# Comparison numbers and W2 of an edge network in PSUM, a table loop in two halves, and one-hot numbers made first

## The chip, the cores and the metric

The kernel runs on one core of a Trainium2 chip. It is written with a tile framework: the program names tiles in SBUF and PSUM and the operations on them, the framework puts each engine's instructions into one static order and sets the semaphores between the engines. The engines are TensorE (PE in the profile, its weight loads PEld), VectorE (DVE), ScalarE (ACT), GpSimd (POOL) and SyncE (SP), and each works through its own list in order. [...]

The metric is the device time of one execution in microseconds (us), taken as a median over executions. The profile is of one further execution, whose own time is given beside it.

## The reference

Four graph networks run one after the other on 6250 nodes of 128 features, each on the layer norm and ReLU of the running sum `x`, and each adds its result to `x`. The graph has 106250 edges, sorted by destination.

```python
def net0(h, norm, rel_emb, W_neighbor, loop_weight, src, dst, edge_type):   # relations, 500 types
    msg = (h[src] + rel_emb[edge_type]) @ W_neighbor
    return relu(segment_sum(msg, dst) * norm + h @ loop_weight)

# net1: three layers; mean over the neighbours, a router takes 2 of 8 experts for every node,
#       h = h + conf * moe; the result is h @ W_out + b_out

def net2(x, src, dst, W1, b1, W2, b2, W4, b4):                              # edge network
    theta = x[dst] - x[src]
    w = sigmoid(relu(theta @ W1 + b1) @ W2 + b2)                            # one number per edge
    agg = segment_sum(w * theta, dst)
    return agg + indegree * (x @ W4 + b4)

# net3: three layers of l2norm(mean over the neighbours) @ Wl.T + bl + l2norm(x) @ Wr.T

x = x + net0(relu(layernorm(x)), ...)
x = x + net1(relu(layernorm(x)), ...)
x = x + net2(relu(layernorm(x)), ...)
x = x + net3(relu(layernorm(x)), ...)
```

## The kernel before

Nodes are padded to 49 tiles of 128, and these are grouped into 13 blocks of four tiles (the last block has one tile). `blk_tiles(b)` is the number of tiles of a block, `P` = `D` = 128, `BW` = 512. Edges are padded to 832 chunks of 128; four chunks make a group, so there are 208 groups (`NWG`) of 512 edges. Since the edges are sorted by destination, the destinations of a group lie in a window of 128 rows (`win(g)`).

**Net 0 and the adjacency.** The kernel first writes the adjacency matrix as bytes into HBM (`adj`), block of destinations by block, from the last block (12) down to block 0. SP clears the blocks from a tile of zeros (`clear`, L310 to L317). VectorE finds for each edge the place of its byte and the number of equal edges: `keys_of(q)` (L398 to L423) loads, on the queue of ScalarE, the source and destination numbers of four index groups of 2048 edges (52 such groups in all), and forms a key for each edge; a copy of the middle of the keys, `own_key`, goes into the PSUM tile `seen`, made by ScalarE (L413). `places(s)` (L425 to L455) compares each key with its neighbours (`req`, L433) and computes the indices `ixs` in a dozen small VectorE instructions. GpSimd then scatters: `scatter(s)` (L457 to L467) issues 16 indirect DMAs of 128 places, one byte each, for one index group, 832 in all, from block 12 down to block 0. The `places` stand in a high-priority part, so the framework puts them early in VectorE's list. TensorE multiplies block b of `adj` with the node rows as soon as SP has loaded it back (`aggregate`, L262 to L282).

Net 0 also needs the counts of edge types. `seen` holds a table of the numbers 0 to 511 (`iota_t`, in bf16): GpSimd makes the numbers (`rnum_i`, L359), VectorE turns them into the bit pattern of small floats (`as_number`, L328) and casts them (L362), TensorE transposes them into `seen` (L364). VectorE compares with it to form one-hot rows (`ohd`, L512, and `oht`, L516). The biases of all networks are loaded by short DMAs on GpSimd's queue (`bias_rows`, L184 to L198): those of `gbias` first; those of net 1's layers belong to net 1's code, and the framework's list has those of the first layer, and some of the second, ahead of the first scatter (L192, between 54 and 79 us in the trace).

**Net 1** takes the adjacency through three layers with gathers and expert multiplies. It isn't touched by the change, but for the place of its bias DMAs on GpSimd's queue.

**Net 2, tables.** A loop over the 13 blocks (L949 to L996) does for each block, in the order of the program: load `rres` (net 1's result, 256 wide) and `rxb`; transpose `rres` on TensorE (L963) and copy it to `roT` (L964); multiply with `W_out` into `rpo` and add a bias row (L968, L970); add it to `rxb` (L971); layer norm of the block's rows into `rh2` (`norm_rows`, L230 to L246, in which VectorE and ScalarE alternate); transpose these (`transposed`, L291, L292); two multiplies per tile, with W1 into `rpg` (L979) and with W4 into `rpv` with a bias row (L980, L981); copy `rpg` to `rgs_o` on ScalarE (L983); write `rh2` and `rgs_o` into the table `tab_s` in HBM (L984, L985); add b1 and split into three bf16 parts (L987, `split3` L123 to L130) for the table `tab_d` (L991); and `rv2` = `rpv` times the in-degree plus `rxb`, which goes to `x_d[1]` (L993 to L996). The framework's list for TensorE keeps this order, so the transposes of a block's `rh2` stand between its `rpo` and its `rpg`.

**Net 2, edges.** For each of the 208 groups (L1089 to L1129) GpSimd gathers four chunks of 128 rows of `tab_s` by source number (L1096, tiles `rss`, six of them in turn). VectorE makes `ohT` (a one-hot of destinations, L1101) and `oh` (L1104, 128x1024, which compares the numbers 0 to 255 of `iota2` with `tloc`); TensorE brings the destinations' rows from the window of `tab_d` (`pz`, L1109); VectorE forms `rz` = `pz` - `rss` and then `max(rz, 0) * W2`:

```python
nc.vector.tensor_tensor(z, pz, ss[:, :, 1 + D:], ALU.subtract)                       # L1111
nc.vector.scalar_tensor_tensor(z, z, 0.0, w2b[:, None, :].to_broadcast([P, WG, D]),  # L1112
                               op0=ALU.max, op1=ALU.mult)
```

ScalarE sums each chunk (L1116) and takes the sigmoid (L1118); ScalarE and VectorE scale the gathered rows into `mv` (L1122, L1123); TensorE adds them into the PSUM tiles `acc` with `oh` (L1129). At the last group of a tile `finish` (L1062 to L1085) turns `acc` into rows of `x` and of the next network. Once enough blocks of these are ready, each group is also followed by one or two steps of `some_sources` (L1043 to L1060): a part of net 3's first multiply, which casts a stretch of `adj` on ScalarE (L1051) and multiplies it on TensorE (L1054, `rpart`). `iota2` (L1026) and `w2b` (L1010) are SBUF tiles. The PSUM pools of this part are `ps_z` 2, `ps_acc` 4 and `ps_a2` 2 tiles, eight banks in all.

**Net 3** is three layers of `aggregate` with small multiplies (L1136 on). It isn't touched.

Of the kernel before, what the change touches and what calls it, by code (L numbers as in the profile page):

```python
# [133 lines left out]
def regular_path(ctx: ExitStack, tc: tile.TileContext, i: dict, out: bass.AP):  # L134
# [167 lines left out]
    with ExitStack() as prep:  # L302
# [6 lines left out]
        pp = pool("rprep", 1)  # L309
        p2 = pool("rprep2", 2)  # L310
        zn = NT * BW // 4
        zero = pp.tile([P, zn // 4], F32, name="rzero")
# [11 lines left out]


        typ_f = pp.tile([P, NCH], F32, name="typ_f")
        dloc_f = pp.tile([P, NCH], F32, name="dloc_f")

        def as_number(dst, k):

            nc.vector.tensor_scalar(dst, k, 16, 1 << 30, op0=ALU.logical_shift_left, op1=ALU.bitwise_or)

        with tc.tile_pool(name="rcols", reuse_waits="tile", bufs=1) as cp:
# [18 lines left out]
            nc.sync.dma_start(dst16, dst_h)  # L352

        ps_k = pool("ps_k", 1, space=bass.MemoryType.PSUM)
        seen = ps_k.tile([P, BW], F32, name="seen")
        iota_t = seen[:, 0:TYP // 2].bitcast(BF16)
        with tc.tile_pool(name="rnum", reuse_waits="tile", bufs=1) as cp:
            num = cp.tile([P, TYT, P], I32, name="rnum_i")
            nc.gpsimd.iota(num, pattern=[[P, TYT], [0, P]], base=0, channel_multiplier=1)  # L359
            as_number(num, num)  # L360
            num_b = cp.tile([P, TYT, P], BF16, name="rnum_b")
            nc.vector.tensor_copy(num_b, num.bitcast(F32))  # L362
            for q in range(TYT):
                nc.tensor.transpose(iota_t[:, q * P:(q + 1) * P], num_b[:, q, :], ident_b)  # L364
        rel3 = pp.tile([P, TYT, 3, D], BF16, name="rel3")
# [32 lines left out]
        def keys_of(q):  # L398
# [13 lines left out]
            own = slice(HALO, HALO + GJ)  # L412
            nc.scalar.copy(own_key[q % 2], key[:, :, own])  # L413
            t1 = p2.tile([P, QG, GJ], I32, name="w_t1")
# [526 lines left out]
    with tc.tile_pool(name="rl2n", reuse_waits="tile", bufs=2) as lp, \  # L941
            tc.tile_pool(name="ps_m2", reuse_waits="tile", bufs=8, space=bass.MemoryType.PSUM) as ps_m:
        w_out = lp.tile([P, 2, D], F32, name="rw_out", bufs=1)
        nc.scalar.dma_start(w_out, rows_of(i["L1_gnn_W_out"], 0, 2))
        w1 = lp.tile([P, D], F32, name="rw1", bufs=1)
        nc.scalar.dma_start(w1, i["L2_gnn_W1"])
        w4 = lp.tile([P, D], F32, name="rw4", bufs=1)
        nc.scalar.dma_start(w4, i["L2_gnn_W4"])
        b1b = lp.tile([P, D], F32, name="rb1b", bufs=1)  # L949
        nc.scalar.dma_start(b1b, bcast_rows(i["L2_gnn_b1"], 0, D))  # L950
        for b in range(NBLK):
            nt = blk_tiles(b)
            w = nt * P
            ts = slice(4 * b, 4 * b + nt)
            res = lp.tile([P, 4, H], F32, name="rres", bufs=4)
            nc.sync.dma_start(res[:, :nt], rows_of(hf_d, 4 * b, nt))
            xb = lp.tile([P, 4, D], F32, name="rxb")
            nc.scalar.dma_start(xb[:, :nt, :], rows_of(x_d[0], 4 * b, nt))
            oT = lp.tile([P, 2, BW], F32, name="roT")
            for f in range(2):  # L960
                p = ps_m.tile([P, 4, P], F32, tag="mm", name="rtr4")
                for t in range(nt):
                    nc.tensor.transpose(p[:, t, :], res[:, t, f * P:(f + 1) * P], ident)  # L963
                nc.scalar.copy(oT[:, f, :w], p[:, :nt, :].rearrange("p t d -> p (t d)"))  # L964
            po = ps_m.tile([P, 4, D], F32, tag="mm", name="rpo")
            for t in range(nt):
                for f in range(2):
                    nc.tensor.matmul(po[:, t, :], oT[:, f, t * P:(t + 1) * P], w_out[:, f, :],  # L968
                                     start=(f == 0), stop=False)
                nc.tensor.matmul(po[:, t, :], sel(1), gbias[:, :D], start=False, stop=True)  # L970
            nc.vector.tensor_tensor(xb[:, :nt, :], po[:, :nt, :], xb[:, :nt, :], ALU.add)  # L971
            norm_rows(h2[:, ts], xb[:, :nt], nt, lp)
            hT = lp.tile([P, BW], F32, name="rhT2")
            transposed(hT, h2, b, ps_m)
            pg = ps_m.tile([P, 4, D], F32, tag="mm", name="rpg")
            pv = ps_m.tile([P, 4, D], F32, tag="mm", name="rpv")
            for t in range(nt):
                tl = hT[:, t * P:(t + 1) * P]
                nc.tensor.matmul(pg[:, t, :], tl, w1, start=True, stop=True)  # L979
                nc.tensor.matmul(pv[:, t, :], tl, w4, start=True, stop=False)  # L980
                nc.tensor.matmul(pv[:, t, :], sel(3), gbias[:, :D], start=False, stop=True)  # L981
            gs = lp.tile([P, 4, D], F32, name="rgs_o")
            nc.scalar.copy(gs[:, :nt], pg[:, :nt])  # L983
            nc.sync.dma_start(rows_of(tab_s, 4 * b, nt)[:, :, 0:D], h2[:, ts, :])  # L984
            nc.sync.dma_start(rows_of(tab_s, 4 * b, nt)[:, :, D:], gs[:, :nt])  # L985
            gd = lp.tile([P, 4, D], F32, name="rgd_o")
            nc.vector.tensor_tensor(gd[:, :nt], gs[:, :nt], b1b[:, None, :].to_broadcast([P, nt, D]), ALU.add)  # L987
            gd3 = lp.tile([P, 4, 3, D], BF16, name="gd3")
            split3(nc, gd3[:, :nt, 0, :], gd3[:, :nt, 1, :], gd3[:, :nt, 2, :], gd[:, :nt],
                   lp, [P, nt, D], "gdr")  # L990
            nc.sync.dma_start(rows_of(tab_d, 4 * b, nt), gd3[:, :nt].rearrange("p t s f -> p t (s f)"))  # L991
            v = lp.tile([P, 4, D], F32, name="rv2")
            nc.vector.tensor_tensor(v[:, :nt], pv[:, :nt],  # L993
                                    deg_r[:, ts][:, :, None].to_broadcast([P, nt, D]), ALU.mult)
            nc.vector.tensor_tensor(v[:, :nt], xb[:, :nt], v[:, :nt], ALU.add)
            nc.scalar.dma_start(rows_of(x_d[1], 4 * b, nt), v[:, :nt])  # L996


# [7 lines left out]
    with tc.tile_pool(name="rl2e", reuse_waits="tile", bufs=2) as ep, \  # L1006
            tc.tile_pool(name="ps_z", reuse_waits="tile", bufs=2, space=bass.MemoryType.PSUM) as ps_z, \
            tc.tile_pool(name="ps_acc", reuse_waits="tile", bufs=4, space=bass.MemoryType.PSUM) as ps_acc, \
            tc.tile_pool(name="ps_a2", reuse_waits="tile", bufs=2, space=bass.MemoryType.PSUM) as ps_a:
        w2b = ep.tile([P, D], F32, name="rw2b", bufs=1)  # L1010
        nc.sync.dma_start(w2b, bcast_rows(i["L2_gnn_W2"], 0, D))
        b2b = ep.tile([P, 1], F32, name="rb2b", bufs=1)
# [11 lines left out]
        nc.vector.tensor_tensor(tloc, dloc.rearrange("p (g k) -> p g k", k=WG), base, ALU.add)  # L1024
        iota2 = ep.tile([P, 2 * P], F32, name="iota2", bufs=1)
        nc.gpsimd.iota(iota2, pattern=[[1, 2 * P]], base=0, channel_multiplier=0,  # L1026
                       allow_small_or_imprecise_dtypes=True)

# [889 lines left out]
```

## Time and profile before

| what | value |
|---|---|
| median of 10 runs | 6431.41 us (6425.83 to 6436.32) |
| profiled execution, its own time | 6435.29 us |
| its span, first to last instruction | 6433.5 us |
| mean granted TensorE clock | 0.879 |
| PE busy, share of the span | 5138.8 us, 80% |
| DVE | 3291.1 us, 51% |
| ACT | 2405.9 us, 37% |
| POOL | 2626.3 us, 41% |

By the starts of its instructions the span falls into these stages. From 0 to about 1250 us: preparation, scatters (the first at 84.64 us, the last at 1164.85) and net 0. From 1250 to 4240: net 1. From 4243 to 4446: the table loop of net 2. From 4446 to about 5643: the edge loop of net 2 (the first gather at 4446.4, the last at 5619.0). From there to 6433: net 3.

The busy shares are averages over these stages, which have different limits; a change is weighed in its own stage, by what each engine waited for there. A group of instructions in the profile names its line, engine and operation, the tile that is written and those read, how often it ran, its busy time and mean duration, and the idle time of its engine just before it with the event that ended it. "issue" means that the engine waited for nothing that the profile shows. Where instructions of one engine are pipelined, their durations overlap a little, so a sum over groups is somewhat more than the engine's busy time.

### The profile page before, as it was taken

The page shows a single profiled execution, that of the slowest core. Times are in us where ns is not written, and L with a number is a line of the kernel's source. Part 1 is how long each engine was busy: PE and PEld are TensorE (multiplying, and loading weights), DVE is VectorE, ACT ScalarE, POOL GpSimd, SP SyncE. Part 2 cuts the span into 40 slices and gives each one's busy share as a digit, 9 for nine tenths or more (in the row PEclk, how much of TensorE's full clock was granted, in tenths as well). Part 3 has the DMA queues.
Part 4 walks back from the last instruction along what each step waited for, and adds up shares of the span by engine and source line. Part 5 has one row for each costly group of instructions (what it writes and reads, how often), then busy time and mean ns, then how long its engine had stood idle before and what let it go on. Part 6 is the DMA issues. An engine that isn't in the chain of part 4 may idle for free. (4 is left out here: it accounts for less than half of the span.)

```text
span 6433.5 us, 84104 instructions
## 1 busy us (share of the span) xinstructions
PE 5138.8 (80%) x28165; PEld 4037.7 (63%) x28189; DVE 3291.1 (51%) x7924; ACT 2405.9 (37%) x5479; POOL 2626.3 (41%) x2376
## 2 busy tenths in 40 slices
PE   0197665899899899988799998855567767879999
PEld 0164443677666688875588885644455555668887
DVE  7987564745311333321233331134777777776565
ACT  2143332433222222212322212223567677824343
POOL 5777777222254111125511113522777777700000
PEclk9998777899899899979899989976678787989999
DMA  8234443544554433235733325553556565624444
GB/s 295 76 62 125 112 107 86 152 141 149 147 100 80 133 100 95 90 108 101 156 90 98 97 82 124 100 142 113 143 163 180 168 178 172 187 64 124 128 146 134
DMA packets 605659, 811.78 MB, mean 126 GB/s; under 512 B 116102, under 2 KB 402616, under 8 KB 605084
## 3 DMA queue, kind: packets, MB, share of 16 engines
q1 hardware_dynamic: 372740, 549.03, 28.0%
q0 software_dynamic: 132896, 194.37, 13.6%
q10 hardware_dynamic: 99448, 61.48, 4.0%
q8 instruction: 267, 4.37, 0.3%
q14 instruction: 308, 2.52, 0.1%
HBM read 594.70 MB, written 209.89 MB: 125 GB/s over the span
## 5 line engine op out<-in xcount | busy, mean ns | idle before, releaser
L793 PE MATMUL ragg<-ra_r,r 128*128 128x512 f32 (+1 forms) x6370 | 1557.5, 406 | 10.1 <-ACT r L763 9.2
L793 PEld LDWEIGHTS ragg<-ra_r,r 128*128 128x128 f32 x6370 | 1232.0, 204 | 264.6 <-ACT r L763 10.0
L1096 POOL DMA_INDIRECT rss<-rtab_s,rsrc_c x832 | 919.7, 1105 | 458.0 <-DMA rx_d<-rv 203.6
L729 POOL DMA_INDIRECT list_d<-rx,rpli x294 | 314.7, 1070 | 1547.2 <-issue 1377.6
L460 POOL DMA_INDIRECT adj<-rcnt,ixs x832 | 809.7, 973 | 277.7 <-issue 237.6
L276 ACT CAST ra_r<-ra_in 128x1024 fp32r<-128x1024 uint8 (+3 forms) x494 | 548.1, 1115 | 841.0 <-PE ragg L279 410.6
L787 DVE CAST ra_r<-ra_in 128x1536 fp32r<-128x1536 uint8 (+4 forms) x507 | 386.7, 765 | 928.6 <-PE ragg L793 858.6
L789 ACT CAST ra_r<-ra_in 128x1024 fp32r<-128x1024 uint8 (+3 forms) x468 | 371.8, 797 | 1147.5 <-PE ragg L793 797.6
L868 POOL DMA_INDIRECT hf_d<-ry,rto x352 | 548.4, 1558 | 579.4 <-DVE ry L854 424.8
L279 PE MATMUL ragg<-ra_r,h 128*128 128x512 f32 (+1 forms) x1274 | 436.2, 434 | 106.1 <-ACT ra_r L276 106.1
L1129 PE MATMUL acc<-mv,oh 128*128 128x258 f32 x1648 | 357.3, 360 | 169.0 <-DVE mv L1123 166.4
L518 PE MATMUL ct<-ohd,oht 128*128 128x128 bf16 (+12 forms) x4096 | 347.6, 215 | 154.3 <-DVE oht L516 144.7
L1129 PEld LDWEIGHTS acc<-mv,oh 128*128 128x128 f32 x1648 | 296.0, 243 | 231.5 <-DVE mv L1123 220.3
L516 DVE TENSOR_SCALAR oht<-seen,typ_f 128x512 bf16<-128x512 bf16 x1024 | 425.8, 473 | 0.0
L518 PEld LDWEIGHTS <-oht 128*128 128x128 bf16 x4096 | 218.7, 100 | 302.6 <-DVE oht L516 220.1
L1109 PE MATMUL pz<-gw,ohT 128*128 128x128 bf16 x2496 | 237.9, 255 | 170.9 <-DVE ohT L1101 98.9
L274 DVE CAST ra_r<-ra_in 128x1024 fp32r<-128x1024 uint8 (+4 forms) x364 | 268.7, 743 | 197.8 <-PE ragg L279 179.8
L1054 PE MATMUL rpart<-ra_r,cur 128*128 128x512 f32 (+1 forms) x1144 | 336.6, 427 | 22.7 <-DVE cur L260 11.6
L279 PE MATMUL ragg<-ra_r,cur 128*128 128x512 f32 (+1 forms) x1404 | 332.1, 395 | 7.7 <-DVE ra_r L274 7.3
L821 DVE COPY at<-rtr 128x512 f32<-128x512 f32 x112 | 77.0, 688 | 497.2 <-PE rtr L820 497.2
L1109 PEld LDWEIGHTS <-ohT 128*128 128x128 bf16 x2496 | 183.7, 116 | 223.4 <-DVE ohT L1101 120.1
L852 PE MATMUL rp<-st,rsh 128*128 128x256 f32 x1344 | 314.9, 383 | 10.7 <-DVE ry L854 10.7
(311 smaller groups left out, 8449.4 us busy)
## 6 DMA issues: line engine op xcount, KB each, us to landing
ra_in<-adj SPq DMA_DIRECT2D x1092, 256.0 KB
row<-list_d SPq DMA_DIRECT2D x111, 516.0 KB
list_d<-rzero SPq DMA_DIRECT2D x65, 774.0 KB
adj<-rzero SPq DMA_DIRECT2D x52, 784.0 KB
rd_b<-dst SPq DMA_DIRECT2D x208, 128.0 KB
gw<-rtab_d SPq DMA_DIRECT2D x208, 96.0 KB
adj<-rcnt,ixs POOLq DMA_INDIRECT x832
rss<-rtab_s,rsrc_c POOLq DMA_INDIRECT x832
```

The costliest lines, as they stand in the source:

```text
L276: nc.scalar.copy(ar[:, m:c, :w], a[:, m:c, :w])
L279: nc.tensor.matmul(ps[:, :w], rows2[:, s, g + k, :], ar[:, k, :w], start=(g + k == t0 and s == 0), stop=(not extra and g + k == NT - 1 and ...
L460: d = nc.gpsimd.indirect_dma_start(out=adj[0:(hi + 1) * ABS], out_offset=bass.IndirectOffsetOnAxis(ap=ixs[:, s, j:j + 1], axis=0), in_=cnt ...
L516: nc.vector.tensor_scalar(oht[:, k, :], iota_t, typ_f[:, c:c + 1], None, op0=ALU.is_equal)
L518: nc.tensor.matmul(ct[:, q, lo:hi], oht[:, k, q * P:(q + 1) * P], ohd[:, k, off:off + hi - lo], start=(n == 0 and k == 0), stop=(n == len( ...
L787: nc.vector.tensor_copy(ar[:, :m, :w], a[:, :m, :w])
L789: nc.scalar.copy(ar[:, m:c, :w], a[:, m:c, :w])
L793: nc.tensor.matmul(ps[:, h_, :w], r2[:, s, g + k, h_ * P:(h_ + 1) * P], ar[:, k, :w], start=(n == 0 and k == 0 and s == 0), stop=(n == len ...
L868: d = nc.gpsimd.indirect_dma_start(out=hf_d[:], out_offset=bass.IndirectOffsetOnAxis(ap=to[:, t:t + 1], axis=0), in_=y[:, t, :], in_offset ...
L1096: nc.gpsimd.indirect_dma_start(out=ss[:, k, 1:], out_offset=None, in_=tab_s[:], in_offset=bass.IndirectOffsetOnAxis(ap=src_c[:, g * WG + k ...
L1109: nc.tensor.matmul(pz[:, k, :], ohT[:, k, :], gw[:, s, :], start=(s == 0), stop=(s == 2))
L1129: nc.tensor.matmul(acc[t], oh[:, k, n * P:(n + 1) * P], mv[:, k].rearrange("p s f -> p (s f)"), start=(g == ends[t][0] and k == 0), stop=( ...
```

## The change

It has three parts and touches three stages.

In the preparation, the block that makes the one-hot numbers moves ahead of the memset of zeros and of the column loads, and stands in a high-priority part; and VectorE, not ScalarE, copies the middle of the keys into `seen`.

In the table loop, W1 and W4 become one tile `w14` of 256 columns, so that each tile of 128 nodes takes one multiply in place of two, with the bias row added to its second half. Its result goes into PSUM tiles for two node tiles each (`rpg`, 2 x 2 x 128), and the copy to `rgs_o` and the multiply by the in-degree run on halves of a block, right behind each such tile. The loop body is cut into `sums(b)`, up to the layer norm, and `tables(b, xb)`, the rest; the loop runs `sums` of a block ahead of `tables` of the block before. `rxb` gets three buffers.

In the edge loop, a new PSUM tile `seen2` (one bank, 3 x 128 floats) holds the 256 numbers and W2; they are made in an SBUF tile `consts` and copied once by VectorE. `oh` and the second `rz` instruction read their constant there. `ps_acc` goes from four buffers to three, which keeps the sum at eight banks. The text of the group loop is unchanged.

```diff
@@ -308,6 +308,23 @@
         nc.sync.dma_start(h[:N - (NT - 1) * P, NT - 1, :], i["x"][(NT - 1) * P:N, :])
         pp = pool("rprep", 1)
         p2 = pool("rprep2", 2)
+
+        def as_number(dst, k):
+
+            nc.vector.tensor_scalar(dst, k, 16, 1 << 30, op0=ALU.logical_shift_left, op1=ALU.bitwise_or)
+
+
+        ps_k = pool("ps_k", 1, space=bass.MemoryType.PSUM)
+        seen = ps_k.tile([P, BW], F32, name="seen")
+        iota_t = seen[:, 0:TYP // 2].bitcast(BF16)
+        with tc.high_priority(), tc.tile_pool(name="rnum", reuse_waits="tile", bufs=1) as cp:
+            num = cp.tile([P, TYT, P], I32, name="rnum_i")
+            nc.gpsimd.iota(num, pattern=[[P, TYT], [0, P]], base=0, channel_multiplier=1)
+            as_number(num, num)
+            num_b = cp.tile([P, TYT, P], BF16, name="rnum_b")
+            nc.vector.tensor_copy(num_b, num.bitcast(F32))
+            for q in range(TYT):
+                nc.tensor.transpose(iota_t[:, q * P:(q + 1) * P], num_b[:, q, :], ident_b)
...
         zn = NT * BW // 4
         zero = pp.tile([P, zn // 4], F32, name="rzero")
         nc.vector.memset(zero, 0.0)
...
-
-        ps_k = pool("ps_k", 1, space=bass.MemoryType.PSUM)
-        seen = ps_k.tile([P, BW], F32, name="seen")
-        iota_t = seen[:, 0:TYP // 2].bitcast(BF16)
-        with tc.tile_pool(name="rnum", reuse_waits="tile", bufs=1) as cp:
-            num = cp.tile([P, TYT, P], I32, name="rnum_i")
-            nc.gpsimd.iota(num, pattern=[[P, TYT], [0, P]], base=0, channel_multiplier=1)
-            as_number(num, num)
-            num_b = cp.tile([P, TYT, P], BF16, name="rnum_b")
-            nc.vector.tensor_copy(num_b, num.bitcast(F32))
-            for q in range(TYT):
-                nc.tensor.transpose(iota_t[:, q * P:(q + 1) * P], num_b[:, q, :], ident_b)
...
             own = slice(HALO, HALO + GJ)
-            nc.scalar.copy(own_key[q % 2], key[:, :, own])
+            nc.vector.tensor_copy(own_key[q % 2], key[:, :, own])
...
-        w1 = lp.tile([P, D], F32, name="rw1", bufs=1)
-        nc.scalar.dma_start(w1, i["L2_gnn_W1"])
-        w4 = lp.tile([P, D], F32, name="rw4", bufs=1)
-        nc.scalar.dma_start(w4, i["L2_gnn_W4"])
+        w14 = lp.tile([P, 2, D], F32, name="rw14", bufs=1)
+        nc.scalar.dma_start(w14[:, 0, :], i["L2_gnn_W1"])
+        nc.scalar.dma_start(w14[:, 1, :], i["L2_gnn_W4"])
...
-        for b in range(NBLK):
+
+        def sums(b):
+
             nt = blk_tiles(b)
             w = nt * P
-            ts = slice(4 * b, 4 * b + nt)
             res = lp.tile([P, 4, H], F32, name="rres", bufs=4)
             nc.sync.dma_start(res[:, :nt], rows_of(hf_d, 4 * b, nt))
-            xb = lp.tile([P, 4, D], F32, name="rxb")
+            xb = lp.tile([P, 4, D], F32, name="rxb", bufs=3)
...
             nc.vector.tensor_tensor(xb[:, :nt, :], po[:, :nt, :], xb[:, :nt, :], ALU.add)
-            norm_rows(h2[:, ts], xb[:, :nt], nt, lp)
+            norm_rows(h2[:, 4 * b:4 * b + nt], xb[:, :nt], nt, lp)
+            return xb
+
+        def tables(b, xb):
+
+            nt = blk_tiles(b)
+            ts = slice(4 * b, 4 * b + nt)
             hT = lp.tile([P, BW], F32, name="rhT2")
             transposed(hT, h2, b, ps_m)
-            pg = ps_m.tile([P, 4, D], F32, tag="mm", name="rpg")
-            pv = ps_m.tile([P, 4, D], F32, tag="mm", name="rpv")
-            for t in range(nt):
-                tl = hT[:, t * P:(t + 1) * P]
-                nc.tensor.matmul(pg[:, t, :], tl, w1, start=True, stop=True)
-                nc.tensor.matmul(pv[:, t, :], tl, w4, start=True, stop=False)
-                nc.tensor.matmul(pv[:, t, :], sel(3), gbias[:, :D], start=False, stop=True)
             gs = lp.tile([P, 4, D], F32, name="rgs_o")
-            nc.scalar.copy(gs[:, :nt], pg[:, :nt])
+            v = lp.tile([P, 4, D], F32, name="rv2")
+            for t in range(0, nt, 2):
+                n = min(2, nt - t)
+                pg = ps_m.tile([P, 2, 2, D], F32, tag="mm", name="rpg")
+                for k in range(n):
+                    nc.tensor.matmul(pg[:, k], hT[:, (t + k) * P:(t + k + 1) * P], w14, start=True, stop=False)
+                    nc.tensor.matmul(pg[:, k, 1, :], sel(3), gbias[:, :D], start=False, stop=True)
+                nc.scalar.copy(gs[:, t:t + n], pg[:, :n, 0, :])
+                nc.vector.tensor_tensor(v[:, t:t + n], pg[:, :n, 1, :],
+                                        deg_r[:, 4 * b + t:4 * b + t + n, None].to_broadcast([P, n, D]), ALU.mult)
             nc.sync.dma_start(rows_of(tab_s, 4 * b, nt)[:, :, 0:D], h2[:, ts, :])
             nc.sync.dma_start(rows_of(tab_s, 4 * b, nt)[:, :, D:], gs[:, :nt])
             gd = lp.tile([P, 4, D], F32, name="rgd_o")
@@ -989,11 +996,16 @@
             split3(nc, gd3[:, :nt, 0, :], gd3[:, :nt, 1, :], gd3[:, :nt, 2, :], gd[:, :nt],
                    lp, [P, nt, D], "gdr")
-            v = lp.tile([P, 4, D], F32, name="rv2")
-            nc.vector.tensor_tensor(v[:, :nt], pv[:, :nt],
-                                    deg_r[:, ts][:, :, None].to_broadcast([P, nt, D]), ALU.mult)
             nc.vector.tensor_tensor(v[:, :nt], xb[:, :nt], v[:, :nt], ALU.add)
             nc.scalar.dma_start(rows_of(x_d[1], 4 * b, nt), v[:, :nt])
+
+        last = None
+        for b in range(NBLK):
+            xb = sums(b)
+            if b:
+                tables(b - 1, last)
+            last = xb
+        tables(NBLK - 1, last)
...
-            tc.tile_pool(name="ps_acc", reuse_waits="tile", bufs=4, space=bass.MemoryType.PSUM) as ps_acc, \
+            tc.tile_pool(name="ps_acc", reuse_waits="tile", bufs=3, space=bass.MemoryType.PSUM) as ps_acc, \
+            tc.tile_pool(name="ps_k2", reuse_waits="tile", bufs=1, space=bass.MemoryType.PSUM) as ps_k, \
             tc.tile_pool(name="ps_a2", reuse_waits="tile", bufs=2, space=bass.MemoryType.PSUM) as ps_a:
-        w2b = ep.tile([P, D], F32, name="rw2b", bufs=1)
-        nc.sync.dma_start(w2b, bcast_rows(i["L2_gnn_W2"], 0, D))
+
+        seen = ps_k.tile([P, 3, P], F32, name="seen2")
+        iota2 = seen[:, 0:2, :].rearrange("p k f -> p (k f)")
+        w2b = seen[:, 2, :]
+        consts = ep.tile([P, 3, P], F32, name="consts", bufs=1)
+        nc.gpsimd.iota(consts[:, 0:2, :], pattern=[[1, 2 * P]], base=0, channel_multiplier=0,
+                       allow_small_or_imprecise_dtypes=True)
+        nc.sync.dma_start(consts[:, 2, :], bcast_rows(i["L2_gnn_W2"], 0, D))
+        nc.vector.tensor_copy(seen, consts)
...
-        iota2 = ep.tile([P, 2 * P], F32, name="iota2", bufs=1)
-        nc.gpsimd.iota(iota2, pattern=[[1, 2 * P]], base=0, channel_multiplier=0,
-                       allow_small_or_imprecise_dtypes=True)
...
```

`as_number` moves up unchanged with the block that uses it.

## The prediction

> **What bounds the kernel now.** Three stages matter, and each was read in its own window: first the groups of instructions, to see which engine paces the stage, then what each engine waited for there, then single instructions in order of time. From the page:
>
> ```profile
> L1096 POOL DMA_INDIRECT rss<-rtab_s,rsrc_c x832 | 919.7, 1105 | 458.0 <-DMA rx_d<-rv 203.6
> L460 POOL DMA_INDIRECT adj<-rcnt,ixs x832 | 809.7, 973 | 277.7 <-issue 237.6
> ```
>
> Both are 832 indirect DMAs on GpSimd, yet a scatter takes 973 ns and a gather 1105. Between two of them lies a gap of 0.30 us that nothing explains ("issue").
>
> Stage A, 0 to 1250 us. The start, and the waits from 500 to 1300 us:
>
> ```profile
> 74.51 0.50 POOL L192 DMA_DIRECT2D bias_f<-in_L_gnn_weak_b  x1
> 75.97 0.20 ACT L413 COPY seen<-w_key 128x64 f32<-128x64 f32 x1
> 77.11 3.44 DVE L433 TENSOR_TENSOR req<-w_key,seen 128x1552 bf16<-128x1552 f32 x2
> ```
>
> ```profile
> ACT ra_r L276 <- DMA ra_in<-adj: 319.1, 9, 59.4
> PE rdr L528 <- ACT rty L523: 205.6, 8, 45.4
> POOL adj L460 <- issue: 146.8, 476, 2.0
> ```
>
> ScalarE waits 319 us for blocks of the adjacency to be loaded, and GpSimd waits for next to nothing: the scatters pace the stage, one per 1.27 us, from 84.64 to 1165.8. The keys (L411, first at 25.87) are there 50 us before ScalarE copies them, since its list has layer norm work first.
>
> Stage B, 4243 to 4446:
>
> ```profile
> POOL rss L1096 <- DMA rx_d<-rv: 203.6, 1, 203.6
> PE rtr L291 <- DVE rh L246: 71.4, 13, 6.6
> DVE rv L993 <- PE rpv L981: 69.1, 11, 6.5
> ACT rgs_o L983 <- PE rpg L979: 47.1, 13, 4.1
> ACT rnr_sq L241 <- DVE rh L237: 41.3, 12, 5.9
> ```
>
> No gather can start until the tables are written, so GpSimd waits the whole stage, while TensorE, VectorE and ScalarE wait for each other in turn: a serial chain, 13 blocks long.
>
> Stage C, 4446 to 5620: waits, then the duration of a gather (minimum, median, maximum), then three instructions:
>
> ```profile
> POOL rss L1096 <- issue: 106.1, 348, 0.3
> DVE rz L1111 <- DMA rss<-rtab_s,rsrc_c: 132.5, 55, 6.6
> ACT rz L1116 <- DVE rz L1112: 175.9, 84, 9.9
> PE acc L1129 <- DVE mv L1123: 156.7, 102, 4.7
> ```
>
> ```profile
> L1096 POOL DMA_INDIRECT rss<-rtab_s,rsrc_c x832: 949/956/2898, 4446.4 to 5619.0; - x167
> ```
>
> ```profile
> 5102.16 0.95 POOL L1096 DMA_INDIRECT rss<-rtab_s,rsrc_c  x1 [0.30 <-DVE rz L1111]
> 5102.90 1.22 DVE L1104 TENSOR_TENSOR oh<-iota,tloc 128x1024 fp32r<-128x1024 f32 x1 [0.81 <-PE acc L1129]
> 5103.42 1.53 POOL L1096 DMA_INDIRECT rss<-rtab_s,rsrc_c  x1 [0.30 <-issue]
> ```
>
> GpSimd is never held longer than the gap (but once), so it paces this stage too. Its typical gather is 956 ns; the mean is lifted by long ones. The last rows show how: the gather at 5103.42 started while `oh` ran, and ended 0.83 us after `oh` did (5104.12 to 4.95). Before it, one of 0.95 started with none such. I went through all 832 this way: the excess over the median sums to 125.8 us (832 x 1.105 - 832 x 0.956 = 124), and by the VectorE instruction that ended 0.83 us earlier it divides into `oh` L1104 80.1 us, `rz` L1112 31.7, `mv` 6.1, `ohT` 2.5 and others about 5. All have only SBUF inputs. `rz` L1111, of the same size but with an input in PSUM, never appears; and in stage A, where the large VectorE inputs lie in PSUM, the scatters' excess is 5.6 us.
>
> **Part A.** Removed from the path: the wait for ScalarE's copy, and the bias DMAs of net 1 in front of the first scatter (two dozen of 0.50 us, up to 78.5); moved: `rnum` to the front of GpSimd's and VectorE's lists. In the changed kernel's order of instructions VectorE does the copy behind the third quarter's key steps (the last such row ends at 34.2), then four `places` with the next compare and `rgbias` (L193 to L198) among them. GpSimd's list has `ecap` ahead of the scatters, which waits for `rgbias` as it does now (20.0 us). Four places took 77.11 to 92.31, 15.2 us; the rest of what stands before `rgbias` some 4. First scatter about 34.3 + 0.2 + 15.2 + 4 = 53.7, near 54.3 against 84.64: -30. The moved layer norm and bias work, some 20 us, fits between places: VectorE makes a group's places in 4.1 us and GpSimd uses them up in 20.3. The net 1 bias DMAs land behind the scatters (12 x 0.5 us), needed at about 1300. Bounds: the clears of blocks 12 and 11 (issued 27.1 to 44.4, DMA busy until 54) could hold the first scatter some 15 us: -12; nothing speaks for more than -34. I take -29.
>
> **Part B.** Today `rxb` (L971) starts every 15.98 us (4249.48 to 4425.3 in 11 steps). On TensorE per block: transposes of `rres` 1.92, `rpo` 2.73, transposes of `rh` 1.09, `rpg` and `rpv` 4.3 (four tiles at 1.07), 10.0 in all, and 5.6 to 6.6 of waiting for `rh`. Merged, a tile is two passes of 128x256: the nearest row is L852, 383 ns each, and a bias pass that adds 0.1: 0.87 at most, 3.3 to 3.5 a block. With `sums` of the next block in front, the norm (0.69 + 0.68 + 0.17 + 0.69 on VectorE, 2.2 on ScalarE, 0.9 back: 5.3) lies beside transposes, `rpo` and multiplies of other blocks (over 8 us). What stays open are the two copies on ScalarE, 0.68 and 0.34. New pitch 9.1 + 1.0 = 10.1. Added: twelve more ScalarE and VectorE instructions of about 0.35, beside it (VectorE is busy 6.4 and ScalarE 5.2 us a block). 11 x (15.98 - 10.1) = 65; the fill of the new order costs 5 us and the last block's single tile gives about as much. I take -66. Bounds: two thirds of the time for the same bytes raise the DMA share from 0.44 to 0.66, as in the last stretch of C; if a table write or ScalarE's two casts of `ra_r` (1.9 us each) delay the chain, pitch 12, -44; a pitch of 9, -78.
>
> **Part C.** `oh` and `rz` L1112 have one input in PSUM, as L1111 has: -111.8 on GpSimd's chain, 1174 to 1062 us. What is late next is VectorE's chain: of its time, 132.5 us waited for gathers, falling from 33.7 in the first 130 us to none in the last 100, where ScalarE is busy 93 of 100 us. Taking for each stretch of 24 groups the larger of GpSimd's freed time (121 us) and the stretch less that wait gives 1087 for 1181, -93. The order is made anew by the framework and three `acc` buffers hold the two live tiles and one more, so I take five off: -88. Bounds: -112 (all of it), and -45 if the freed waits come back half on ScalarE's and TensorE's side (their waits above are as large). VectorE: 691 ns for PSUM with SBUF (L971), 681 for two SBUF inputs (L246): 10 ns x 416 = 4 us, hidden, as VectorE is busy 149 of the 200 us from 4500 (busy time by stretches).
>
> [...] The rows, 691 against 681, decide for -88. [...]
>
> **The sum.** -29 - 66 - 88 = -183 against the profiled execution's own 6435.3 (span 6433.5, 1.8 outside): 6252. That execution lies 3.9 above the median of the runs, so 6248 for the median. A measurement can tell 0.2%, 13 us, from no change.
>
> **Rivals.** (1) Stage C's consumers take over sooner: against it, VectorE idles a quarter of the stage; for it, their mutual waits. C -45: 6291. (2) Stage B's lists don't interleave as the program does, because ScalarE has the next block's copies behind this block's norm: B -30: 6284. [...] (4) Slower: reading the constant from PSUM makes `oh` and `rz` L1112 (1.91 us a group) slow, and VectorE paces C. It is busy 4.3 of 5.64 us a group; A and B (95 us, 0.46 a group) are eaten up at 6.10, when those two take 1.94 times as long. At twice: (6.2 - 5.64) x 208 = 116, net +21: 6452. Against it stand L971, and `ohd` from `seen` at 0.68.
>
> **How the numbers follow.** Mine 0.58, (1) 0.15, (2) 0.10, (1) with (2) or with a late first scatter 0.07, about 6325, (3) 0.06, (4) 0.04. From 6207 (all three lower bounds: -34, -78, -112) to 6330 (-12, -44, -45) leaves out (3), (4) and a few hundredths of tails. Mine alone: 6220 to 6275. Faster: all but (4), 0.94; within 0.2%: 0.02; slower 0.04.
>
> **What would show it.** First scatter near 54 us, last near 1136; `rxb` starts 10 us apart and first gather about 130 us after the first of them, now 197; gathers' mean under 0.98 us and 5.1 to 5.2 us for four; VectorE's wait for gathers below 50 us, `oh` still 1.2 us. Wrong would be: long gathers still ending 0.83 us after `oh`; `rxb` 13 us apart or more; a longer `oh`.

## The result and the profile after

The changed kernel takes 6223.87 us (6217.9 to 6231.01), the kernel before in the same comparison 6432.75: a ratio of 0.9675, with a 95% interval of 0.9667 to 0.9684, or 209 us less (203 to 214). The forecast was 6248, range 6207 to 6330. The profiled execution took 6217.16 us (span 6215.3) and lies 7 us below its median; against the profiled execution of before it is 218.1 shorter. Cut at the same instructions as in the table of stages, these divide as follows:

| stage, from and to | before, us | after, us | difference | forecast |
|---|---|---|---|---|
| A: start to the first multiply of net 1's gather rows (`ragg` from `r`) | 1251.0 | 1232.4 | -18.6 | -29 |
| net 1, to the first transpose of `rres` | 2992.6 | 2986.8 | -5.8 | 0 |
| B: to the first gather | 202.8 | 111.0 | -91.8 | -66 |
| C: to the last multiply into `acc` | 1194.6 | 1095.3 | -99.3 | -88 |
| the rest, to the end | 792.4 | 789.8 | -2.6 | 0 |

Net 1's code is the same in all kernels here, but for the place of its bias loads; over ten profiled executions of them it took 2973 to 2993 us, so the -5.8 means nothing. All three parts gained. The page's lines for the two kinds of indirect DMA, then the durations of a gather (minimum, median, maximum):

```profile
L1113 POOL DMA_INDIRECT rss<-rtab_s,rsrc_c x832 | 809.1, 972 | 374.0 <-DMA rx_d<-rv 111.9
L459 POOL DMA_INDIRECT adj<-rcnt,ixs x832 | 813.1, 977 | 270.0 <-issue 242.7
```

```profile
L1113 POOL DMA_INDIRECT rss<-rtab_s,rsrc_c x832: 950/957/1559, 4330.2 to 5400.4; - x167
```

The mean gather fell from 1105 ns to 972 at the same median (956 and 957): the long ones are gone. GpSimd's wait for the tables fell from 203.6 to 111.9 us. The waits in stage C of the changed kernel (what waited, for what; total us, times, longest):

```profile
ACT rz L1133 <- DVE rz L1129: 122.7, 68, 8.7
...
PE acc L1146 <- DVE mv L1140: 109.8, 76, 5.4
POOL rss L1113 <- issue: 98.5, 323, 0.3
...
DVE rz L1128 <- DMA rss<-rtab_s,rsrc_c: 22.0, 13, 5.7
```

VectorE's wait for gathers fell from 132.5 to 22.0 us, and the large waits of the others fell with it: ScalarE's for `rz` from 175.9 to 122.7, TensorE's for `mv` from 156.7 to 109.8. One that grew is TensorE's for ScalarE's cast (`rpart` for `ra_r`), from 10.1 to 42.8. GpSimd still paces the stage, at 5.1 us for four gathers in the first 192 groups (5.6 before).

In stage B the waits, of the changed kernel:

```profile
DVE rv L989 <- ACT rgs_o L988: 19.1, 14, 2.9
...
PE rtr L291 <- DVE rh L246: 3.9, 2, 3.2
```

TensorE's wait for the normed rows, 71.4 us before, is 3.9. The table of busy time by stretches (stretch, its length, busy us and instructions of PE, PEld, DVE, ACT and POOL, then the granted clock, the DMA share and GB/s) shows what came with it. The loop before, as a whole:

```profile
4243.00:4446.00 203.00, 119.26 (x661) 102.80 (x661) 83.49 (x153) 67.07 (x192) 0.00 (x0) 0.70 0.44 129
```

and the loop after, whole, and 20 us from its middle:

```profile
4215.00:4330.00 115.00, 88.85 (x563) 70.33 (x563) 80.37 (x163) 65.84 (x204) 2.90 (x2) 0.89 0.78 231
4275.00:4295.00 20.00, 16.38 (x112) 12.86 (x110) 15.20 (x32) 13.13 (x46) 0.00 (x0) 1.00 0.81 233
```

TensorE's granted clock went from 0.70 to 0.89 over the whole loop, and is 1.00 in its middle, where stretches of 20 us of the loop before show 0.61 to 0.74. The blocks start 7.84 us apart, not 10.1.

### The profile page after: what moved, and what is told of

The parts are those of the page before. It is cut to its first block, busy times and chain, and to the rows that moved or that the text cites. A ratio compares the mean times of both kernels' runs of the same rounds, so it can differ in the third digit from the quotient of the medians.

```text
span 6215.3 us, 84003 instructions
## 1 busy us (share of the span) xinstructions
PE 5075.8 (82%) x28067; PEld 3985.1 (64%) x28091; DVE 3289.5 (53%) x7950; ACT 2413.3 (39%) x5478; POOL 2524.1 (41%) x2376
## 5 line engine op out<-in xcount | busy, mean ns | idle before, releaser
L1113 POOL DMA_INDIRECT rss<-rtab_s,rsrc_c x832 | 809.1, 972 | 374.0 <-DMA rx_d<-rv 111.9
L1146 PE MATMUL acc<-mv,oh 128*128 128x258 f32 x1648 | 352.6, 357 | 111.2 <-DVE mv L1140 109.8
L1071 PE MATMUL rpart<-ra_r,cur 128*128 128x512 f32 (+1 forms) x1144 | 323.6, 409 | 48.6 <-ACT ra_r L1068 42.8
L1126 PE MATMUL pz<-gw,ohT 128*128 128x128 bf16 x2496 | 253.5, 262 | 123.1 <-DVE ohT L1118 67.6
L279 PEld LDWEIGHTS ragg<-ra_r,h 128*128 128x128 f32 x1274 | 228.1, 201 | 163.3 <-ACT ra_r L276 146.3
```

What stands on the lines that cost most here:

```text
L279: nc.tensor.matmul(ps[:, :w], rows2[:, s, g + k, :], ar[:, k, :w], start=(g + k == t0 and s == 0), stop=(not extra and g + k == NT - 1 and ...
L1071: nc.tensor.matmul(ps[:, :w], cur2[:, s, g + k, :], ar[:, k, :w], start=(g + k == t0 and s == 0), stop=(g + k == t1 - 1 and s == 1))
L1113: nc.gpsimd.indirect_dma_start(out=ss[:, k, 1:], out_offset=None, in_=tab_s[:], in_offset=bass.IndirectOffsetOnAxis(ap=src_c[:, g * WG + k ...
L1146: nc.tensor.matmul(acc[t], oh[:, k, n * P:(n + 1) * P], mv[:, k].rearrange("p s f -> p (s f)"), start=(g == ends[t][0] and k == 0), stop=( ...
```

## The experiments

**Each part alone.** Part A alone is the kernel before with the diff's hunks ahead of the table loop; part B alone has those of the loop; part C alone those behind it. The fourth kernel is part C with its operands put back:

```diff
         nc.vector.tensor_copy(seen, consts)
+        iota2 = consts[:, 0:2, :].rearrange("p k f -> p (k f)")
+        w2b = consts[:, 2, :]
```

> Part A alone on the kernel before. Theory: the gain is the earlier first scatter and nothing else, so the first scatter stands near 61.6 us as in the changed kernel, the last near 1143, and the time falls by 18 to 24 us (ratio 0.996 to 0.997). Rival, that the missing third of part A's forecast (-29) is lost to the other parts: 29 us or more. Rival, that net 1's biases, now behind the scatters, cost something in net 1: less than 15 us of gain.

> Part B alone. Theory: the table loop is faster by itself, its blocks 7.8 us apart, with a granted clock near 1.0 in the middle of it: -92 us (ratio 0.9857, within 0.985 to 0.987). Rival, that the clock there is high only because of what ran before it in the changed kernel: blocks about 10 us apart, -66 us (0.990).

> Part C alone. Theory: gathers no longer lengthened by the one-hot comparison and the multiply by W2: excess over the median of the 832 gathers 14 us in place of 126, four gathers every 5.1 us, -99 us (ratio 0.9846, within 0.983 to 0.987). Rival, that part of stage C's gain comes from the tables being written sooner or from the other parts: -88 or less (0.986 or more).

> Everything of part C but the operands: the constants are made and copied to PSUM as in the change, three buffers for the sums, but the comparison and the multiply read the SBUF copy. Theory (the operand's place is the cause): no gain, 0.998 to 1.002, and the gathers' excess is back at about 125 us. Rival (the new order of instructions or the smaller pool did it): ratio 0.985 to 0.993.

| kernel | ratio to before | interval | us of 6432 |
|---|---|---|---|
| part A alone | 0.9976 | 0.9965 to 0.9987 | -15 |
| part B alone | 0.986 | 0.9843 to 0.9876 | -90 |
| part C alone | 0.9849 | 0.9833 to 0.9866 | -97 |
| part C, operands in SBUF | 1.0002 | 0.9992 to 1.0011 | +1 |

The three ratios multiply to 0.9688; the whole measured 0.9675. The 8 us between them lie within the three intervals, so nothing shows that the parts help or hinder each other. Part A gave less than the 18 to 24 us expected; what it lost is in the next section. Its stage has to be compared on one chip: from the first to the last scatter it took 1089 to 1094 us in these four kernels, and 1078 to 1079 in the next four, which ran on another. Of the first four, net 1's first multiply comes at 1246.1 us in the one with part A and at 1259.3 to 1260.2 in the others. The pages' lines of the gathers, of part C alone and then of part C with its operands in SBUF:

```profile
L1101 POOL DMA_INDIRECT rss<-rtab_s,rsrc_c x832 | 809.3, 973 | 469.8 <-DMA rx_d<-rv 204.5
```

```profile
L1103 POOL DMA_INDIRECT rss<-rtab_s,rsrc_c x832 | 919.9, 1106 | 458.3 <-DMA rx_d<-rv 204.0
```

Same pools, same copy to PSUM, same code but for two operands: 973 or 1106 ns, and 97 us or nothing. So the place of the operands carries all of part C, and three `acc` buffers and the new order of instructions carry none of it. The excess of the gathers over their median, divided by the VectorE instruction that ended 0.83 us earlier as in the prediction, is 15 us in part C alone, and 126.0 with the operands in SBUF (84.0 of it beside `oh`, 28.5 beside `rz`).

**One operand at a time.** Part C with `w2b` from `consts`, and with `iota2` from `consts`:

> Part C with only the comparison numbers in PSUM; the multiply reads W2 from SBUF. Theory: the gathers' excess falls by what the comparison held, 126 to 40 us, and the time by 75 to 82 us (ratio 0.987 to 0.9885). Rival (after the first operand the consumers are the bound): the time falls by all of part C, 94 us or more (0.985).

> Part C with only W2 in PSUM; the comparison reads its numbers from SBUF. Theory: the multiply's share of the excess goes, 126 to about 95 us, and the time falls by 25 to 32 us (ratio 0.995 to 0.996). Rival (gathers freed from the multiply are caught by the next comparison instead): excess 115 or more, the time within 10 us of before.

With the comparison numbers in PSUM the ratio was 0.9886 (0.9869 to 0.9902), 73 us, and the excess 47 us; with W2 alone 0.9965 (0.9952 to 0.9978), 22 us, and the excess 100 us. Both gains are a little under the expected ones (75 to 82 and 25 to 32). Together they are 95 us, against 97 for both operands: each operand frees its own share of the 126, and neither rival holds (a consumer that takes over after the first operand, or the next comparison catching what the multiply lets go).

**Part B's two halves.** The order alone keeps two multiplies per tile and whole-block copies; the merge alone calls the two functions in the old order:

```diff
-        last = None
-        for b in range(NBLK):
-            xb = sums(b)
-            if b:
-                tables(b - 1, last)
-            last = xb
-        tables(NBLK - 1, last)
+        for b in range(NBLK):
+            tables(b, sums(b))
```

> Only the order of part B: sums of a block ahead of tables of the block before, three rxb buffers; the multiplies with W1 and W4 stay two, their copies stay whole blocks. Theory (the wait for the norm is what the order removes, and a TensorE that no longer waits is granted more clock): blocks 8.5 to 9.5 us apart, granted clock 0.9 or more in the middle of the loop, first gather 75 to 90 us sooner (ratio 0.986 to 0.989). Rival (TensorE's durations stay those of before, 10.0 us a block, and 1.0 of copies): blocks 11 us apart, -55 us (0.9915).

> Only the other half of part B: W1 and W4 in one tile, copies by halves, the loop in the order of before. Theory: the chain stays serial, TensorE waits for each norm as before (71 us) and its clock stays near 0.7; saved are about 1 us of multiplies per block and a part of a copy, so blocks 14.0 to 15.0 us apart, -13 to -25 us (ratio 0.996 to 0.998). Rival (the merge, not the order, carries the gain): blocks under 12 us apart, more than -50 us.

The order alone: 0.9866 (0.9848 to 0.9884), 86 us; its first gather comes 122.8 us after the first transpose, for 202.8 before and 109.5 with both halves, and its blocks start 9.0 us apart. A stretch from its loop, with the clock third from the end:

```profile
4255.00:4275.00 20.00, 16.12 (x127) 14.74 (x128) 13.79 (x24) 10.94 (x34) 0.00 (x0) 0.95 0.99 299
```

The merge alone: 0.9999 (0.999 to 1.0009); first gather after 198.7 us, blocks 15.4 apart. This is a miss: blocks 14 to 15 us apart and a gain of 13 to 25 us were expected. The waits of the merge alone:

```profile
DVE rv L990 <- ACT rgs_o L989: 77.2, 25, 4.7
PE rtr L291 <- DVE rh L246: 68.9, 13, 6.5
```

The second of them, TensorE waiting for the norm, is nearly as long as before (71.4), and the granted clock stays at 0.72 and 0.70 in two stretches of the loop. What a multiply saves goes into a chain in which TensorE waits anyway. In the new order, where TensorE's own list is the limit, the same merge shortens the loop by 122.8 - 109.5 = 13 us, for 4 in the old one. This is read from the profiles, in which the loop before takes 202.7 to 204.2 us in all six kernels that keep it; the times, 86 us and 90, don't tell the two apart. Which edit pays depends on what the other left as the bound.

**A heavier and a lighter comparison; an earlier scatter.** Two kernels do the comparison twice per group, into the same tile: first from an SBUF copy, or both from PSUM. A third moves two things in the preparation of the changed kernel (the scratch of the first biases keeps its own memory, and GpSimd numbers `rbase` earlier), and a fourth is the changed kernel itself.

```diff
+        iota_s = consts[:, 0:2, :].rearrange("p k f -> p (k f)")
...
+            nc.vector.tensor_tensor(oh, iota_s[:, None, :].to_broadcast([P, WG, 2 * P]),
+                                    tloc[:, g, :, None].to_broadcast([P, WG, 2 * P]), ALU.is_equal)
             nc.vector.tensor_tensor(oh, iota2[:, None, :].to_broadcast([P, WG, 2 * P]),
```

```diff
-    with tc.tile_pool(name="gb", reuse_waits="tile", bufs=1) as gp:
+    l1 = ExitStack()
+    gp = l1.enter_context(tc.tile_pool(name="gb", reuse_waits="tile", bufs=1))
...
-            nc.gpsimd.iota(base, pattern=[[241, NWG], [0, WG]], base=0, channel_multiplier=0)
+            with tc.high_priority():
+                nc.gpsimd.iota(base, pattern=[[241, NWG], [0, WG]], base=0, channel_multiplier=0)
```

> The changed kernel with the one-hot comparison done twice per group into the same tile: first from an SBUF copy of the numbers, then from PSUM as in the change. This adds 208 VectorE instructions of 1.22 us with two SBUF inputs and nothing else. Theory (a gather that starts beside such an instruction is held): the gathers' excess rises from 14 to 90 us or more, four gathers take 5.5 us, the time is 75 to 110 us over the changed kernel's (ratio to the kernel before 0.979 to 0.985).

> The same with both comparisons reading PSUM: the same added VectorE time (254 us), one input in PSUM. Theory: the gathers' excess stays under 20 us; VectorE is then busy 5.3 to 5.5 of each group's time and paces the stage at about 5.5 us a group, so the time is 50 to 85 us over the changed kernel's, less than with the SBUF copy. [...]

> The changed kernel with two small moves in the preparation: the scratch of the first bias rows keeps its own memory, so the three index tables of net 1 on GpSimd's list need not wait for it, and the numbers of the windows (rbase) are made before VectorE forms the first keys. Theory: the first gives 10 to 12 us, since the first scatter's indices are ready at 49.4 and it starts at 61.6; the second lets VectorE's first key instruction end 2 us sooner, so that the third load of edge numbers is issued ahead of the clears and lands at 33.6, not 39.5. First scatter at 43 to 46 us, time 14 to 18 us below the changed kernel's. Rival (the clears of block 12 are not landed by then): first scatter at 50 us or later, under 11 us.

> The changed kernel once more, beside the last one on the same chip: ratio to the kernel before 0.966 to 0.969.

These four ran on one chip on which every kernel takes far longer: the kernel before 7313.79 us (7291.9 to 7328.91, 30 runs). There the changed kernel gains nothing: 7330.39 us, ratio 1.0023 (1.0013 to 1.0033). So none of the four times can be read as expected; the section on the hardware comes back to this. Three readings that rest on single instructions still stand.

First, the gathers. With the extra comparison from SBUF, and with both from PSUM, from the two pages:

```profile
L1114 POOL DMA_INDIRECT rss<-rtab_s,rsrc_c x832 | 901.7, 1084 | 619.2 <-DVE mv L1143 297.8
```

```profile
L1113 POOL DMA_INDIRECT rss<-rtab_s,rsrc_c x832 | 814.1, 978 | 769.6 <-DVE mv L1142 437.8
```

VectorE does the same added work in both, 208 comparisons. The excess is 108.7 us in the first (89.8 of it beside `oh`) and 18.8 in the second, and 17.0 in the changed kernel on this chip; 90 or more and under 20 were expected. It isn't VectorE's load that lengthens gathers but an instruction with both inputs in SBUF. The expected times for these two (75 to 110 and 50 to 85 us over the changed kernel) weren't met: the first was 46 us faster than the changed kernel (7284.01), the second equal to it (7329.63).

Second, the changed kernel's first scatter started at 55.65 us on this chip and at 61.56 in the profile after; the next section uses this. Third, the earlier scatter: its first started at 53.83, and what it waited for last was not VectorE's indices but a DMA. The profile names a load that SP issued right behind the clears, which the scatter doesn't read; what it does need of that queue are the clears of block 12:

```profile
POOL adj L461 <- DMA rdst_c<-in_dst_cols: 16.5, 1, 16.5
```

So the rival holds here, as far as the profile tells: block 12 isn't cleared much sooner, and under 2 us were gained at the start. Whether it helps on the other chips wasn't measured, and the time (7327.29, ratio 1.0019, 1.0009 to 1.0028) gives no reason to prefer it.

## Why the prediction was right, and by how much it wasn't

**Part C: right, -88 forecast, -97 alone, -99 in the stage.** The step "`oh` and `rz` L1112 have one input in PSUM, as L1111 has: -111.8 on GpSimd's chain" held nearly to the number: the excess fell from 125.8 to 14.1. From the first to the last gather the stage lost 102.3 us (1172.6 to 1070.3). What was mis-sized is the deduction: the forecast took off 19 us for VectorE's chain and five for the new order and smaller pool. The order and the pool cost nothing (+1 us measured), and the consumers took back some 12: the last 16 groups, with ScalarE busy 184 of the 200 us ahead of 5400, went at 5.7 us in place of 5.1, and the work behind the last gather took 25.1 us for 22.1. That the constant's place in PSUM costs VectorE nothing held as well: `oh` 1224 ns median for 1225, `rz` 677 for 683. The pair of rows that it was taken from is less clean than it looks: the 681 ns of L246 are its mean in the edge loop, and in the table loop, where L971's 691 come from, L246 takes 692 too.

**Part B: right in kind, too small: -66 forecast, -90 alone, -92 in the stage.** The order did what was said. The failed term is "New pitch 9.1 + 1.0 = 10.1": the 9.1 were durations of TensorE at a low clock. The 0.70 of the loop before is a mean of stretches at 0.50 and at 1.00. Its trace has the same eight transposes at both, one row at a granted clock of 1.00, and the row that the forecast took, at 0.53:

```profile
4262.04 1.04 PE L963 MATMUL rtr<-rident,rres 128*128 128x128 f32 x8
...
4324.99 1.92 PE L963 MATMUL rtr<-rident,rres 128*128 128x128 f32 x8
```

They take 1.04 us in four of the twelve full blocks before, and in every block from the third on after. In the new order TensorE hardly waits for the norm (3.9 us in all), the clock is 1.00 in the middle of the loop, and four transposes of `rh` take 0.61 us there for 1.09. The sum of the timeline of one block is 2.22 (`rpg`) + 1.04 + 0.76 (wait for `roT`) + 2.53 (`rpo`) + 0.61 + 0.68 (wait for `rhT`) = 7.84, which is the pitch. TensorE's own part of it is 6.4 us for the 9.1, and the copies that stay open are 1.4 for the 1.0. The order alone shows the clock too, with 0.95, 0.88 and 0.91 in three stretches of its loop. Over the whole loop it was 0.70 in the profile before, where TensorE waited 71.4 us for the norm, and 0.89 after, with 3.9 us of waiting; the forecast's sum has no term for such a change. What sets the clock isn't shown.

**Part A: right in kind, too large: -29 forecast, -15 alone, -18.6 in the stage.** The first scatter came at 61.56, not 54.3. The step that failed is "VectorE does the copy behind the third quarter's key steps (the last such row ends at 34.2)". The order is as it says, but the time was read from the trace of before, and in the changed kernel these steps wait for a load until 39.53. VectorE's list in the profile after, then GpSimd's:

```profile
25.76 2.83 DVE L414 TENSOR_SCALAR w_t<-w_dst 128x64 int32<-128x64 int32 x1
25.88 2.71 DVE L410 SCALAR_TENSOR_TENSOR w_key<-w_low,w_src 128x448 f32<-128x448 int32 x1
...
39.53 0.20 DVE L416 TENSOR_SCALAR w_t<-w_src 128x64 int32<-128x64 int32 x1 [5.71 <-DMA w_src<-in_src_ext]
...
40.00 0.22 DVE L412 COPY seen<-w_key 128x64 f32<-128x64 f32 x1
```

```profile
25.96 2.57 POOL L350 IOTA rbase<- 128x832 int32 x1
...
60.47 0.24 POOL L580 IOTA ecap<- 128x64 f32 x1 [31.74 <-DVE rgbias L198]
...
61.56 1.08 POOL L459 DMA_INDIRECT adj<-rcnt,ixs  x1 [0.61 <-issue]
```

The first key instruction took 2.71 us here. It was caught beside GpSimd's numbering of `rbase` and ended only with it, at 28.59. The buffer of edge numbers that it reads comes free then, so the third load was issued at 28.65, behind the clears that SP had begun at 27.11, and landed at 39.5. In the trace that the forecast was read from, the numbering ran beside the key as well, but didn't hold it, and the third load was issued at 26.53, ahead of the clears:

```profile
25.87 0.62 DVE L411 SCALAR_TENSOR_TENSOR w_key<-w_low,w_src 128x448 f32<-128x448 int32 x1
...
26.18 2.15 POOL L339 IOTA rbase<- 128x832 int32 x1
```

That trace was the exception. Of the ten profiles ahead of the last four kernels, the key took 2.3 to 2.7 us in eight, and in part C alone it began only at 28.34; in all nine but before, the third quarter's steps began at 39.2 to 39.9 us, in part A alone too (39.91, first scatter at 61.94). On the chip of the last four kernels, in the three that keep the changed kernel's preparation, it was as in the trace of before. The changed kernel there:

```profile
25.63 0.62 DVE L410 SCALAR_TENSOR_TENSOR w_key<-w_low,w_src 128x448 f32<-128x448 int32 x1
...
33.62 0.19 DVE L416 TENSOR_SCALAR w_t<-w_src 128x64 int32<-128x64 int32 x1
```

Its first scatter was at 55.65, close to the 54.3 of the forecast. So bad luck with the one trace of before made up some six of the seven us by which the first scatter was late. What decides whether the key is held stays open: the numbering began 0.08 us behind it in the profile after, 0.31 behind it in the trace of before, and 0.54 behind it in part B alone, where the key took 2.43 us. From the copy to the first scatter it took 21.6 us, for 20.0 forecast. The prediction's "one per 1.27 us" is 1.30 on average over the scatters of before (84.64 to 1164.85); nothing rests on it.

The rest is lost at the end, in a step that was costed at nothing ("The net 1 bias DMAs land behind the scatters (12 x 0.5 us), needed at about 1300"). The DMAs cost nothing, but VectorE's five instructions on each of these biases moved too, and now stand in the last layer norm of net 0, between its mean and its reciprocal. After (the mean, two of the bias instructions, the reciprocal), then before:

```profile
1219.43 0.16 DVE L217 TENSOR_SCALAR rln_nm<-rln_s 128x4 f32<-128x4 f32 x1
...
1223.42 0.43 DVE L193 CAST rbias<-bias_f 128x512 bf16<-128x512 f32 x1 [3.24 <-DMA bias_f<-in_L_gnn_conf_b]
...
1226.90 0.68 DVE L198 TENSOR_TENSOR rbias<-bias_f,bias_mid 32x512 bf16<-32x512 f32 x1
1227.61 0.18 DVE L225 RECIPROCAL rln_r<-rln_sd 128x4 f32<-128x4 f32 x1
```

```profile
1241.78 0.16 DVE L217 TENSOR_SCALAR rln_nm<-rln_s 128x4 f32<-128x4 f32 x1
...
1246.66 0.17 DVE L225 RECIPROCAL rln_r<-rln_sd 128x4 f32<-128x4 f32 x1
```

8.2 us from mean to reciprocal in place of 4.9, with VectorE idle for 3.24 of the 8.2 while it waited for a bias DMA that this norm doesn't need. From the last scatter to net 1's first multiply it took 89.3 us, and 90.6 in part A alone, for 85.3 to 87.2 in the eight kernels with the old part A.

**The rivals.** Neither (1), consumers that take over, at its size, nor (2), lists that don't interleave, nor (3), gathers held as before with the constants in PSUM (their excess fell to 14.1 us), nor (4), slow reads from PSUM, came about. By the stages, two terms of the sum were too small (B by 26, C by 11) and one too large (A by 10), 27 together; the forecast stood 24 above the median.

## What to carry to other kernels

When gathers that GpSimd issues pace a loop, look for gathers longer than the median and for the VectorE instruction that ended just before them; a constant operand moved to PSUM freed them here (their excess fell from 125.8 us to 14.1) at no cost to VectorE (`oh` 1224 ns for 1225). Durations of TensorE read from a loop full of waits can be those of a low granted clock, as here (eight transposes 1.92 us at 0.53 and 1.04 at 1.00): look for the same rows at 1.00 before adding them up. When an edit removes the waits, TensorE's instructions can get shorter too (here four transposes of `rh` from 1.09 to 0.61 us), and an edit that only removes multiplies may be worth nothing until the waits are gone (here a ratio of 0.9999 alone, and 13 us of the loop behind the new order). A time at the start of a kernel that is read from one profile can be the exception: read it from several. A step that is moved takes all its instructions along, on every engine, and they can land inside a chain that had nothing to do with it.

## What the runs showed of the hardware

**GpSimd and VectorE.** Which of the two is held depends on how far `oh` is when a gather begins. In the trace of before, 164 gathers began while `oh` (two SBUF inputs) ran, long enough before its end for a delay to show. 143 of them ended 0.83 us after it. Another 20 began within about 0.03 us of `oh`; these took their usual time, and `oh` took 1.26 to 1.29 us in place of 1.22:

```profile
5114.95 1.27 DVE L1104 TENSOR_TENSOR oh<-iota,tloc 128x1024 fp32r<-128x1024 f32 x1 [1.12 <-PE acc L1129]
5114.97 0.95 POOL L1096 DMA_INDIRECT rss<-rtab_s,rsrc_c  x1 [0.30 <-issue]
```

So VectorE is held in turn as well, but little: of the 208 rows of `oh` (1204 to 1286 ns, median 1225) 22 are longer, by 0.9 us in all. After the change, with the constant in PSUM, `oh` took 1206 to 1226 ns, and none of the 174 such gathers ended late with it. Other work of GpSimd held VectorE for longer: beside the numbering of `rbase` the key instruction took 2.71 us in the profile after, for 0.62 in that of before, and one with a single SBUF input (L414, 128x64), begun 0.12 us ahead of the key, took 2.83 for 0.19.

**A chip on which the gain is gone.** On the chip of the last four kernels, TensorE and ScalarE nearly stood still while GpSimd issued scatters, and VectorE was slowed. The same 200 us of the same kernel, in the profile after and on that chip (columns as above):

```profile
700.00:900.00 200.00, 109.09 (x962) 74.62 (x964) 102.77 (x240) 57.86 (x61) 149.71 (x155) 0.75 0.35 98
```

```profile
700.00:900.00 200.00, 1.29 (x20) 0.91 (x20) 56.80 (x144) 0.00 (x0) 154.15 (x143) 1.00 0.02 0
```

TensorE ran 20 instructions there for 962, and VectorE 144, about as many as GpSimd's scatters (143). The timeline shows them waiting for something that the profile can't name ("remote"), and going on just after a scatter ended:

```profile
808.37 1.10 POOL L459 DMA_INDIRECT adj<-rcnt,ixs  x1 [0.30 <-issue]
809.51 0.18 DVE L447 SCALAR_TENSOR_TENSOR rix<-rrel_b,w_low 128x16 int32<-128x16 int32 x1 [3.58 <-remote]
...
811.17 1.09 POOL L459 DMA_INDIRECT adj<-rcnt,ixs  x1 [0.30 <-issue]
812.30 0.95 DVE L436 TENSOR_REDUCE rv<-req 128x16 f32<-128x768 bf16 x1 [2.54 <-remote]
```

Net 0's work then runs mostly after the last scatter (1216.3), and net 1 begins at 1929.5 and not 1232.4. In stage C GpSimd waits 438.8 us for VectorE's `mv`, so it no longer paces that stage (1460 us from the first to the last gather, for 1070), which fits that freeing it gained nothing; VectorE's `oh` alone waits 176.8 us for "remote" there. The kernel whose extra comparison holds gathers back was even 46 us faster; why isn't shown. The table loop, in which GpSimd was busy 0.37 of 112 us, is as short there as elsewhere (110.8 us, for 111.0 in the profile after). What stalls the engines on that chip, and why its kernel before is no slower than the changed one although the table loop should still have gained, stays open: there is no profile of the kernel before on it, and nothing here tells how common such chips are.
